# Narrower filler products at the start of a conditioned sequence kernel, and sixty filler products among its last chains

## The chip, the cores and the metric

The kernel runs on one core of a Trainium2 chip. The core has five engines, each with its own in-order queue: TensorE (PE, with weight loads shown apart as PEld), VectorE (DVE), ScalarE (ACT), GpSimd (POOL) and SyncE (SP, which here issues the DMAs). The metric is the device time of one execution in microseconds (us), lower is better.

## The reference

Four layers follow each other on x of 8 batches by 512 tokens by 256 channels, all in float32:

```python
# layer 0: a conditioned transformer block, 16 heads of 16, feed-forward of 1024
emb = jax.nn.silu(_sin_emb(timestep)) @ W_ada + b_ada
scale, shift = jnp.split(emb[:, None, :], 2, axis=-1)
x = _ln(src) * (1.0 + scale) + shift
q, k, v = (heads(x @ W + b) for W, b in ((Wq, bq), (Wk, bk), (Wv, bv)))
scores = jnp.einsum('bhqd,bhkd->bhqk', q / math.sqrt(HEAD_DIM), k) + attention_bias
scores = jnp.where(src_mask, -jnp.inf, scores)
ctx = jnp.einsum('bhqk,bhkd->bhqd', jax.nn.softmax(scores, axis=-1), v)
x = x + (ctx @ Wo + bo)
h = _ln(x) * g2 + beta2
x = x + _gelu2(h @ W1 + b1) @ W2 + b2
# layer 1 and layer 3: adapters of width 64 with an expert chosen by the batch's domain
hidden = gelu(x @ down_W.T + down_b)
hidden = hidden @ expert_W[idx].T + expert_b[idx] + domain_emb[idx]
x = _ln(hidden @ up_W.T + up_b + x) * ln_gamma + ln_beta
# layer 2, between the adapters: pairs of channels turned by the angles theta and phi
```

(`heads` stands for the split into 16 heads. The attention bias, 8 x 16 x 512 x 512 values, is the largest input, 134 MB.)

## The kernel before

The work of each batch is a preparation (layer norm, q, k and v of 512 tokens), 16 attention units (4 groups of four heads by 4 tiles of 128 queries), and a `finish` for tokens (output product, feed-forward, the two adapters with the rotation between them). `finish` takes two tiles of 128 tokens at a time; the last two tiles of the last batch go one by one.

The kernel does not emit instructions as it goes. Each step is given to a `Plan` as a task: an engine (or several to choose from), an estimated cost in us, a function that emits it, what it reads and writes, and a rank. At the end `plan.run` plays the tasks through a model of the engines: whenever an engine is free it takes the ready task of the lowest rank whose buffers can be had. The order so found is the order of every engine's queue; on the chip the engines then wait for each other by semaphores. A filler task therefore fills what the plan believes to be an idle stretch, and stands in PE's queue ahead of whatever comes next. `Buffer(BG)` takes one of four PSUM banks for background work (it may borrow one of the four banks of the scores) and holds it from its first task to its last.

Two places matter here.

At the start, `embedding` (L411) gives PE 42 filler products of the identity with itself at rank -2.45, behind the real work of the first microseconds in rank: L421. Each loads a 128 x 128 weight tile and streams the 128 columns of the same tile. The real work among them is, in PE's order: the tokens spread over the partitions (L429, ready after a small input has landed), a shift of the bias columns (L515), the product of the embedding with w_ada (L484, `product`, four records of 512 columns), the transposes of the first batch (L807), four small transposes of the modulation (L498), then q and k (L827) and the first scores (L936). Five fillers stand before L429, 14 between L515 and L484, 3 before L807, 7 before L827, 6 before the first scores and 7 behind them.

At the end, three `finish` chains overlap: the last batch's tiles 0 and 1 together (A), tile 2 (B) and tile 3 (C). An adapter is a chain of short steps that go from engine to engine: transposes (PE, L751), a copy (L709, ACT or DVE), the down product (PE, L1122), the gelu (ACT, L1130), the up product (PE, L775), the addition (DVE, L1139), statistics (DVE L717 and L719, ACT L731, POOL L724 to L726), the normalized rows (ACT, L739), and either the rotation (DVE L1162, L1158, L1173) or the last scale and shift (DVE, L1149) and the store (L1202). A float32 product leaves two records on PE, each with its own weight load; a transpose leaves one.

Of the kernel before, what the change touches and what calls it, by code (L numbers as in the profile page):

```python
# [20 lines left out]
P = 128  # L21
# [4 lines left out]
NF = FF // P  # L26
# [19 lines left out]
PE, DVE, ACT, POOL, DMA = "PE", "DVE", "ACT", "POOL", "DMA"  # L46
# [202 lines left out]
def conditioned_sequence_kernel(  # L249
# [22 lines left out]
    nc = tc.nc  # L272
# [14 lines left out]
    BG = Slots(banks[4:], SC)  # L287
# [69 lines left out]
    ident = shifted[:, HD:]  # L357
# [28 lines left out]
    plan = Plan()  # L386
# [24 lines left out]
    def embedding():  # L411

        tiny = Buffer(GT)
        tokf = lambda: tiny.t[:1, 0, : 2 * B]
        scr = Buffer(BG, lambda t: t[:, :128].rearrange("p (r n) -> p r n", r=4))

        plan.rank = -2.45
        warm = Buffer(BG, lambda t: t[:, :P])

        def rows_of_identity():  # L420
            nc.tensor.matmul(warm.t, ident, ident, start=True, stop=True)  # L421

        for i in range(42):
            plan(PE, 0.22 if i > 6 else 0.48, rows_of_identity, [], [warm], mode="full")
        plan.rank = -12.0

        plan.rank = -21.0
        plan(DVE, 0.2, lambda: nc.vector.tensor_copy(tokf(), tok_i), [], [(tiny, 0)], at=3.2)
        plan(PE, 0.3, lambda: nc.tensor.matmul(  # L429
            scr.t[:, 0, : 2 * B], ones, tokf(), start=True, stop=True), [(tiny, 0)], [scr],  # L430
            mode="full")

        def reduced():
            turns, last = scr.t[:, 2, : B + 2], scr.t[:, 3, : B + 2]
            red = tiny.t[:, 1, : B + 2]
            nc.vector.tensor_scalar(
                ang[:, :B], scr.t[:, 0, :B], 40.0, cols[:, C_FREQ : C_FREQ + 1], ALU.mult,
                ALU.mult,
            )
            nc.vector.tensor_scalar(turns, ang, float(1.0 / (2.0 * np.pi)), None, ALU.mult)  # L440
            nc.vector.tensor_scalar(turns, turns, ROUND, ROUND, ALU.add, ALU.subtract)
            nc.vector.scalar_tensor_tensor(red, turns, -TWO_PI_HI, ang, ALU.mult, ALU.add)
            nc.vector.scalar_tensor_tensor(red, turns, -TWO_PI_LO, red, ALU.mult, ALU.add)
            nc.vector.tensor_scalar(last, red, PI_IN, -PI_IN, ALU.min, ALU.max)

        plan(DVE, 1.2, reduced, [], [scr, (tiny, 1)], at=4.0)

        def sines():
            red = scr.t[:, 3, : B + 2]
            nc.scalar.activation(sc[:, 0], red, AF.Sin)  # L450
            nc.scalar.activation(sc[:, 1], red, AF.Sin, scale=0.5)
            nc.scalar.activation(sc[:, 1], sc[:, 1], AF.Square)
            nc.scalar.activation(sc[:, 1], sc[:, 1], AF.Identity, bias=1.0, scale=-2.0)

        plan(ACT, 0.9, sines, [scr], ["sc"])

        th = Buffer(BG, lambda t: t[:, : NC * B].rearrange("p (c b) -> p c b", c=NC))
        plan(ACT, 0.25, lambda: nc.scalar.activation(
            th.t, sc[:, :, :B], AF.Tanh, scale=0.5), ["sc"], [th])
        plan(DVE, 0.2, lambda: nc.vector.scalar_tensor_tensor(  # L460
            emb, th.t, 1.0, sc[:, :, :B], ALU.add, ALU.mult), [th, "sc"], ["emb"])
        plan.rank = -11.5

        def chosen():
            domf, clip = scr.t[:A, 0, B : 2 * B], tiny.t[:A, 2, :B]
            nc.vector.tensor_scalar(clip, domf, 0.0, float(E - 1), ALU.max, ALU.min)
            nc.vector.tensor_tensor(valid, domf, clip, ALU.is_equal)
            nc.vector.tensor_tensor(invalid, domf, clip, ALU.not_equal)
            nc.vector.tensor_copy(expert_i, clip[:1])

        plan(DVE, 0.6, chosen, [], [scr, (tiny, 2), "valid", "expert"])
# [264 lines left out]
    def normed(dst, dst_keys, src, src_keys, ts, rstd):  # L736

        for t, key, dkey in zip(ts, src_keys, dst_keys):
            plan(ACT, 0.5, lambda t=t: nc.scalar.activation(  # L739
                dst(t), src.t[:, t, :], AF.Identity, bias=rstd.t[:, 1, t : t + 1],  # L740
                scale=rstd.t[:, 0, t : t + 1]), [rstd, key], [dkey])
# [305 lines left out]
    def feed_forward(res, rk, ts, store=None):  # L1047
        hat = Buffer(TMP)
        at = {t: i for i, t in enumerate(ts)}
        n, w = len(ts), len(ts) * P  # L1050
        here = slice(ts[0], ts[0] + n)

        hk = [(hat, i) for i in range(n)]
        normed(lambda t: hat.t[:, at[t], :], hk, res, rk, ts, statistics(res, rk, ts))
        hT, hk = half_transposed(
            lambda t: hat.t[:, at[t], :], hk, ts, C_G2, C_BETA2
        )
        gT = Buffer(GT) if store is None else store
        for f2 in range(NF // 2):
            ps = Buffer(BG, lambda t: t.rearrange("p (i q) -> p i q", i=2))  # L1060
            sg = Buffer(SIG)
            for i in range(2):
                f = 2 * f2 + i

                def hidden(i=i, f=f, ps=ps):
                    for c in range(NC):
                        nc.tensor.matmul(  # L1067
                            ps.t[:, i, :w], w1[:, c, f * P : (f + 1) * P], hT.t[:, c, :w],
                            start=(c == 0), stop=(c == NC - 1),
                        )  # L1070

                plan(PE, 0.432 * n, hidden, [*hk, "w1"], [(ps, i)], mode="full")

            for i in range(2):
                f = 2 * f2 + i
                plan(ACT, 0.155 + 0.1 * n, lambda i=i, f=f, ps=ps, sg=sg: nc.scalar.activation(  # L1076
                    sg.t[:, i, :w], ps.t[:, i, :w], AF.Tanh, bias=b1s[:, f : f + 1],
                    scale=0.851), [(ps, 0), (ps, 1), "b1s"], [(sg, i)])
            plan(POOL, 0.05 + 0.27 * n, lambda sg=sg: nc.gpsimd.tensor_scalar(  # L1079
                sg.t[:, :, :w], sg.t[:, :, :w], 0.5, 0.5, ALU.mult, ALU.add), [], [(sg, 0), (sg, 1)])  # L1080
            for i in range(2):
                f = 2 * f2 + i
                plan(DVE, 0.14 + 0.13 * n, lambda i=i, f=f, ps=ps, sg=sg: nc.vector.scalar_tensor_tensor(  # L1083
                    gT.t[:, f, :w], ps.t[:, i, :w], cols[:, C_B1 + f : C_B1 + f + 1],
                    sg.t[:, i, :w], ALU.add, ALU.mult), [(ps, i), (sg, i)], [(gT, f)])
        ps = Buffer(BG, lambda t: t.rearrange("p (i d) -> p i d", i=2))
        for i in range(n):
            for f0 in range(0, NF, 2):

                def out_sums(i=i, f0=f0):  # L1090
                    for f in (f0, f0 + 1):
                        nc.tensor.matmul(  # L1092
                            ps.t[:, i, :], gT.t[:, f, i * P : (i + 1) * P], w2[:, f, :],
                            start=(f == 0), stop=(f == NF - 1),
                        )

                plan(PE, 0.86, out_sums, [(gT, f0), (gT, f0 + 1), "w2"], [ps], mode="full")
        plan(DVE, 0.3 * n, lambda: nc.vector.tensor_tensor(
            res.t[:, here], ps.t[:, :n], res.t[:, here], ALU.add), [ps], rk)

    eus, rots = {}, {}

    def adapter(b, l, res, rk, ts):
        n, w = len(ts), len(ts) * P
# [104 lines left out]
    def experts_matrices():  # L1209
# [70 lines left out]
        for b in range(B) for half in range(2) for g in range(NG) for i in range(2)  # L1280
    ]
    embedding()
    modulation()
    constants()
# [5 lines left out]
    for n, u in enumerate(units):  # L1290
        if n % 16 == 0 and u[0] + 1 < B:
            plan.begin()
            prepare(u[0] + 1)
            plan.end(n + 0.5, n + 13.0)
        attention(u, n)
        if n % 8 == 7:
            half = n // 8 % 2
            if n + 1 < len(units):
                plan.begin()
                finish(u[0], [2 * half, 2 * half + 1])  # L1300
                plan.end(n + 2.0, n + (11.0 if n < 100 else 19.0))
                continue

            for t in range(2):
                plan.begin()
                finish(u[0], [2 + t], Buffer(PT, lambda p: p.rearrange(
                    "p (c q) -> p c q", q=2 * P)[:, :NF]) if t else None)
                plan.end(n + 2.0 + 4 * t, n + 11.0 + 4 * t)
    plan.stir([
        (691236, 48.0, 53.0, 0.3),  # L1310
        (61640, 125.7, 135.7, 0.15),
# [135 lines left out]
```

## Time and profile before

| what | us |
|---|---|
| median of 3 runs (lowest to highest) | 879.17 (878.11 to 880.26) |
| the profiled execution's own time | 876.14 |
| its span, first to last instruction | 874.3 |
| mean granted TensorE clock over the span | 0.991 |
| start of L484's first record, end of its chain piece | 10.35, 12.23 |
| start of the first scores (L936) | 19.51 |
| start of the last transposes (L751), down product (L1122), up product (L775) | 863.71, 864.86, 866.42 |
| end of the last DVE operation (L1149) | 871.49 |

The granted clock is the share of TensorE's clock pulses that are let through; it is recorded when it changes, and 1.00 stands where nothing was recorded. In this execution it is recorded as full from 9.52, half from 132.40 to 135.81, full again, and half from 862.85 on. PE matmul records overlap: a record of 128 columns lasts 0.27 us at full clock while the next starts 0.11 behind it, so spacings and not durations tell the pace. A row of the timeline merges equal instructions that follow each other without a gap, with their number as "xN" and, in brackets, the idle time before the first and what ended it.

### The profile page before, as it was taken

Reading aid. Unit: us, or ns where it says so; the run is one execution under the profiler, and the core shown is the slowest. Engines: PE = TensorE matmul, PEld = TensorE weight load, DVE = VectorE, ACT = ScalarE, POOL = GpSimd, SP = SyncE. Lnnn points to the kernel's source line nnn. Section 1 sums busy time; section 2 is a strip of 40 time slices with the busy share of each in tenths; the row PEclk is TensorE's granted clock in tenths of the full one; section 3 lists DMA queues with packets and bytes.
Section 4 is the critical chain, followed back from the end, with each engine's and each line's share of the span. In section 5 each row is a group of like instructions: output and inputs, shape, how many; then the busy total and the mean of one; then the engine's idle time right before and its main releaser. Section 6 shows DMA issues by size and latency. Waiting matters only on the chain.

```text
span 874.3 us, 20269 instructions
## 1 busy us (share of the span) xinstructions
PE 852.1 (97%) x6430; PEld 564.5 (65%) x6430; DVE 784.2 (90%) x2147; ACT 737.1 (84%) x1343; POOL 775.3 (89%) x907
## 2 busy tenths in 40 slices
PE   9999999999999999999999999999999999999994
PEld 7656665667666665667656666666756576666783
DVE  3778998989999989999999989999989899999766
ACT  5997869989898889979899898989989898799653
POOL 8699999989899989999999998998979998999432
PEclk9999999999999999999999999999999999999997
DMA  9689796698888889798897979979887988998300
GB/s 304 208 297 306 262 283 200 200 298 258 281 279 271 263 253 314 217 285 277 286 295 226 301 225 275 314 228 294 269 284 232 279 259 281 299 322 264 98 25 24
DMA packets 163936, 221.56 MB, mean 253 GB/s; under 512 B 18819, under 2 KB 93613, under 8 KB 163782
## 3 DMA queue, kind: packets, MB, share of 16 engines
q1 hardware_dynamic: 163786, 220.25, 79.9%
q8 instruction: 51, 0.84, 0.4%
q14 instruction: 55, 0.45, 0.2%
q10 hardware_dynamic: 44, 0.02, 0.0%
HBM read 152.92 MB, written 7.27 MB: 183 GB/s over the span
## 4 chain that ended last, share of the span: by engine, by line
PE 66%; ACT 13%; POOL 10%; DVE 4%; DMA 3%; issue 3%; SPq 0%; POOLq 0%; DVEq 0%; ACTq 0%
PE bank L936 11%; PE bank L987 10%; PE bank L1092 10%; PE bank L1013 9%; PE bank L1067 8%; POOL bias L928 8%; PE bank L775 5%; PE bank L827 4%; ACT bias L952 4%; DMA bias<-in_bias 3%; PE bank L865 3%; PE bank L751 2%; PE bank L421 2%; PE bank L1122 1%; DVE bias L948 1%
## 5 line engine op out<-in xcount | busy, mean ns | idle before, releaser
L928 POOL TENSOR_TENSOR bias<-bias,neg 128x512 f32<-128x512 f32 x512 | 580.2, 1163 | 10.6 <-DMA bias<-in_bias 9.7
L952 ACT ACTIVATE bias<-bias,low 128x512 f32<-128x512 f32 x512 | 344.9, 719 | 43.7 <-DVE low L948 42.9
L948 DVE CUSTOM_DVE_ANT_0 bias<-bank,bias 128x512 f32<-128x512 f32 x512 | 329.0, 679 | 28.6 <-PE bank L936 21.6
L987 PEld LDWEIGHTS bank<-shifted,bias 128*128 128x128 f32 x1120 | 126.0, 141 | 70.6 <-ACT bias L952 26.0
L963 DVE STREAM_TRANSPOSE tb<-bias 128x512 f32<-128x512 f32 x232 | 156.8, 695 | 7.5 <-ACT bias L952 7.3
L987 PE MATMUL bank<-shifted,bias 128*128 128x128 f32 x1120 | 158.7, 277 | 1.9 <-ACT pT L709 0.7
L936 PE MATMUL bank<-kT,qz 32*128 32x512 f32 x1024 | 146.3, 641 | 3.9 <-DVE low L948 3.8
L709 ACT COPY pT<-bank 128x512 f32<-128x512 f32 x215 | 120.5, 582 | 30.3 <-PE bank L987 29.5
L1067 PE MATMUL bank<-hT,w 128*128 128x256 f32 (+1 forms) x544 | 127.0, 374 | 1.7 <-ACT hT L761 1.2
L1013 PE MATMUL bank<-pT,v_pad 128*32 128x256 f32 x1120 | 123.4, 382 | 0.0
L1092 PE MATMUL bank<-w,gT 128*128 128x256 f32 x496 | 119.9, 383 | 0.0
L1067 PEld LDWEIGHTS bank<-hT,w 128*128 128x128 f32 x544 | 94.1, 190 | 29.5 <-issue 9.0
L1013 PE MATMUL bank<-pT,v_turn 128*32 128x256 f32 x928 | 111.4, 382 | 0.0
L1092 PEld LDWEIGHTS bank<-w,gT 128*128 128x128 f32 x496 | 89.5, 190 | 21.4 <-issue 9.9
L1013 PEld LDWEIGHTS bank<-pT,v_turn 128*32 128x32 f32 x928 | 48.9, 109 | 51.6 <-issue 8.0
L936 PEld LDWEIGHTS bank<-kT,qz 32*128 32x128 f32 x1024 | 40.0, 182 | 43.6 <-DVE low L948 15.0
L1076 ACT ACTIVATE sig<-bank,b1s 128x256 f32<-128x256 f32 (+1 forms) x136 | 55.5, 455 | 8.7 <-PE bank L1067 7.4
L1083 DVE SCALAR_TENSOR_TENSOR gT<-bank,cols,sig 128x256 f32<-128x256 f32 (+1 forms) x128 | 54.2, 464 | 6.5 <-POOL sig L1079 5.9
L1079 POOL TENSOR_SCALAR sig<-sig 128x512 f32<-128x512 f32 (+1 forms) x68 | 40.4, 595 | 20.1 <-ACT sig L1076 17.7
L1013 PEld LDWEIGHTS bank<-pT,v_pad 128*32 128x32 f32 x1120 | 54.8, 109 | 4.4 <-issue 0.8
L717 DVE BATCH_NORM_STATS2 st<-res 128x6 f32<-128x256 f32 x128 | 51.4, 411 | 1.6
L709 DVE COPY pT<-bank 128x512 f32<-128x512 f32 x65 | 43.3, 674 | 5.4 <-ACT bias L952 3.0
(138 smaller groups left out, 1112.5 us busy)
## 6 DMA issues: line engine op xcount, KB each, us to landing
bias<-in_bias SPq DMA_DIRECT2D x512, 256.0 KB
pT<-tb SPq DMA_DIRECT2D x464, 128.0 KB
out<-res SPq DMA_DIRECT2D x15, 256.0 KB
res<-in_x SPq DMA_DIRECT2D x7, 512.0 KB
value_rows<-v_pad SPq DMA_DIRECT2D x8, 272.0 KB
v_turn<-value_rows SPq DMA_DIRECT2D x8, 272.0 KB
m<-in_mask SPq DMA_DIRECT2D x8, 256.0 KB
mod<-ada_rows SPq DMA_DIRECT2D x8, 256.0 KB
```

The source lines that it names most:

```text
L709: nc.scalar.copy(*pair()) if e == ACT else nc.vector.tensor_copy(*pair())), r, w)
L928: plan(POOL, 1.12, lambda j=j: nc.gpsimd.tensor_tensor(dif[j].t, dif[j].t, negs[qt].t, ALU.add), [negs[qt]], [dif[j]])
L936: nc.tensor.matmul(sc[j].t, qz.t[strip, par, c, qs], kT.t[strip, c, :], start=True, stop=True,)
L948: plan(DVE, 0.61, lambda j=j: nc.vector.tensor_tensor_reduce(dif[j].t, sc[j].t, dif[j].t, -1.0, 3.0e38, ALU.add, ALU.min, low.t[:, j : j + ...
L952: plan(ACT, 0.62, lambda j=j: nc.scalar.activation(dif[j].t, dif[j].t, AF.Exp, bias=low.t[:, j : j + 1], scale=-1.0), [(low, j)], [dif[j]] ...
L963: plan(DVE, 0.62, lambda j=j: nc.vector.transpose(tb.t.rearrange("p (m h k c) -> h p k m c", m=4, h=TURNED, k=NT)[j], dif[j].t.rearrange(" ...
L987: nc.tensor.transpose(ps.t[:, kc, :], dif[j].t[:, kc * P : (kc + 1) * P], ident)
L1013: nc.tensor.matmul(pv.t[32 * j : 32 * j + 32, :], (v_turn if j < turned else v_pad).t[:, at : at + 32], pj, start=(kc == 0), stop=(kc == N ...
L1067: nc.tensor.matmul(ps.t[:, i, :w], w1[:, c, f * P : (f + 1) * P], hT.t[:, c, :w], start=(c == 0), stop=(c == NC - 1),)
L1076: plan(ACT, 0.155 + 0.1 * n, lambda i=i, f=f, ps=ps, sg=sg: nc.scalar.activation(sg.t[:, i, :w], ps.t[:, i, :w], AF.Tanh, bias=b1s[:, f : ...
L1083: plan(DVE, 0.14 + 0.13 * n, lambda i=i, f=f, ps=ps, sg=sg: nc.vector.scalar_tensor_tensor(gT.t[:, f, :w], ps.t[:, i, :w], cols[:, C_B1 + ...
L1092: nc.tensor.matmul(ps.t[:, i, :], gT.t[:, f, i * P : (i + 1) * P], w2[:, f, :], start=(f == 0), stop=(f == NF - 1),)
```

## The change

The fillers 7 to 19 of the 42 at the start stream 64 columns of the identity instead of 128, with the same weights and the same planned cost. At the end of the plan, 60 products of the identity with 64 of its columns are added, with the highest rank of all (200.0) and a planned cost of 0.11, ready once the last feed-forward (chain C) has written the last of its activations. They share one bank.

```diff
-        def rows_of_identity():
-            nc.tensor.matmul(warm.t, ident, ident, start=True, stop=True)
+        def rows_of_identity(w):
+            nc.tensor.matmul(warm.t[:, :w], ident, ident[:, :w], start=True, stop=True)
 
         for i in range(42):
-            plan(PE, 0.22 if i > 6 else 0.48, rows_of_identity, [], [warm], mode="full")
+            w = P // 2 if 6 < i < 20 else P
+            plan(PE, 0.22 if i > 6 else 0.48, lambda w=w: rows_of_identity(w), [], [warm],
+                 mode="full")
...
         gT = Buffer(GT) if store is None else store
+        inner.append(gT)
...
-    eus, rots = {}, {}
+    eus, rots, inner = {}, {}, []
...
+    still = Buffer(BG, lambda t: t[:, : P // 2])
+
+    def half_of_identity():
+        nc.tensor.matmul(still.t, ident, ident[:, : P // 2], start=True, stop=True)
+
+    plan.rank = 200.0
+    for _ in range(60):
+        plan(PE, 0.11, half_of_identity, [(inner[-1], NF - 1)], [still], mode="full")
```

In the changed program's queues, PE's real instructions stand in the same order as before, and so do those of DVE, ACT, POOL and SP; only the banks of the last chains differ. Between L515 and the w_ada product stand two full and twelve narrow fillers, behind it one narrow and two full. The sixty stand as follows among the last products (line numbers of the kernel before):

```
L751  transposes of A (adapter 1), then of C (adapter 0)
   7 fillers
L1122 down product of C, then of A
   1
L775  up product of C;  L751 transposes of B (adapter 1)
   2
L775  up product of A;  L1122 down product of B
   6
L775  up product of B
  25
L751  transposes of C (adapter 1)
   7
L1122 down product of C
   6
L775  up product of C
   6
```

## The prediction

> **What bounds the kernel now.** First view: the page's engine totals and slices. TensorE (PE) is busy 97% of a span of 874.3 us and nines in 39 of 40 slices; what delays PE's first real work or its last chain shows in the end time, and little else does.
>
> ```profile
> PE 852.1 (97%) x6430; PEld 564.5 (65%) x6430; DVE 784.2 (90%) x2147; ACT 737.1 (84%) x1343; POOL 775.3 (89%) x907
> PEclk9999999999999999999999999999999999999997
> ```
>
> Second view: the chain of waits in the first 24 us (start, length, what; "xN" counts PE records, and a float32 product leaves two, each with its own weight load).
>
> ```profile
> 1.40 2.50 PE bank L421 x10
> 3.90 0.53 PE bank L429 x2
> 4.44 0.53 PE bank L515 x2
> 4.96 5.46 PE bank L421 x28
> 10.42 1.81 PE bank L484 x4
> ...
> 18.24 1.34 PE bank L421 x12
> ```
>
> The fillers (L421) themselves are the chain: the last input of the product at L484, `emb`, is written by DVE at 7.26 to 7.41, yet L484 follows the 14 fillers at 10.42. They are slow there: a window of 1 us holds 6 filler records at 5.2 and at 8.2 but 11 at 14.5, so a record takes 0.2133 us on the half clock and 0.1117 (18.24: 1.34/12) on the full one. The clock column reads 1.00 before its first change, so durations must tell: the records' starts close up at 9.52. From there it holds until 132.40, falls to half for exactly 3.41 us, and falls again at 862.85. Those times lie a whole number of steps of 3.413 us apart, so I read the clock as decided once per such window, with edges at 2.69, 6.11, 9.52, 12.93. Third view, busy time by window (columns: PE, PEld, DVE, ACT, POOL, clock, DMA):
>
> ```profile
> 2.69:6.11 3.42, 3.42 (x16) 3.16 (x16) 2.40 (x12) 1.79 (x6) 3.09 (x12) 1.00 0.87 231
> 6.11:9.52 3.41, 3.41 (x18) 3.41 (x18) 1.54 (x12) 1.78 (x9) 2.22 (x7) 1.00 1.09 375
> 128.99:132.40 3.41, 1.55 (x12) 0.71 (x11) 2.87 (x8) 2.60 (x6) 3.33 (x6) 1.00 0.90 285
> 753.63:757.04 3.41, 2.26 (x20) 1.29 (x17) 3.38 (x9) 3.41 (x7) 3.17 (x4) 1.00 0.98 310
> ```
>
> The first kept PE "busy" throughout and its weight loads 92%, and did not raise the clock; 1.06 us of it (3.90 to 4.96) were the narrow products L429 and L515. The second, full of wide fillers, did. The third lost the clock, the fourth kept it. Counting a record's moving columns at 0.83 ns each (128 take the 0.1067 that L807's spacing of 0.109 contains), doubled while cold, the moving side streams 65%, 100%, 36% and 56% of these four windows.
>
> Fourth view, the last chain in the timeline (start, length):
>
> ```profile
> 857.53 0.30 PEld L775 LDWEIGHTS bank<-eu,hid 65*128 65x128 f32 x2 [0.26 <-ACT hid L1130]
> 858.22 0.20 PEld L751 LDWEIGHTS bank<-shifted,res 128*128 128x128 f32 x2 [0.39 <-DVE res L1173]
> 863.71 0.69 PE L751 MATMUL bank<-shifted,res 128*128 128x128 f32 x2 [2.36 <-DVE res L1173]
> 864.86 1.11 PE L1122 MATMUL bank<-hT,wd 128*64 128x128 f32 x4 [0.46 <-ACT hT L709]
> 866.42 1.22 PE L775 MATMUL bank<-eu,hid 65*128 65x256 f32 x2 [0.45 <-ACT hid L1130]
> ```
>
> PE waits 2.36, 0.46 and 0.45 us for DVE and ACT, and at half clock its last product takes 1.22 where the same one took 0.70 at 860.65.
>
> **The price of a narrow filler.** A filler loads 128 weight columns and streams 128 (before) or 64. Which side sets the pace? Weight loads of this plain kind take 190 ns (L1067, 128 columns), 137 (L686, 64), 109 (L1013, 32), 88 (L484, 8): 83 ns plus 0.83 per column, so a load occupies its path 107 ns for 128 columns. In the tail, two L775 loads of 0.19 fit in 0.30 (the second 0.11 behind); two transposes' loads (L751, 142 ns) in 0.20, 0.06 behind. Through the whole trace no plain full-height load of 128 columns is followed sooner than 0.108. So the filler's weights already set its 0.1117 (the transposes L807, whose loads are quicker, reach 0.109). Halving the moving side should leave 0.1117 warm (0.223 an instruction) and 0.2133 cold. The cold rows agree: L429 and L515 stream 16 and 8 columns behind 128 weight columns, and their loads last 308 and 310 ns. The other bound is half, 0.112 an instruction (L1267: 64 by 64, eight records in 0.63). I take the first: the filler's weight load is L1067's, not L1267's.
> The Trainium skill (TensorE: Matmul & The Clock Gate, Back-to-back issue gap) gives an isolated product with 1 to 64 moving columns about 60 cycles, half its figure for 128; by it the narrow filler halves. The same passage adds that in a stream of load and product pairs both sides set the spacing.
>
> **The change, part by part.**
> *Order.* All engines keep the order of their real instructions to the end; PE alone gets new instructions, no DMA moves or is added. Two full and twelve narrow fillers stand before the w_ada product, one narrow and two full behind it. The bank that the 60 hold shifts the tail's other banks. The waits that this brings end before they are met (on PE: DVE's reads of a shared bank, done at 857.70 and, in the sum below, 859.7, with PE there at 858.6 and 860.5; on ACT: copies that end by 856.5): nothing.
> *Start, issue time.* 28 records stay 28 cold records: 4.96 + 28 x 0.2133 = 10.93.
> *Start, clock.* The narrow ones stream 64 columns of each 0.1117 (0.2133 cold): 48 to 50%. 65% was not enough, so I expect no rise at 9.52, where the last wide records gained the 0.5 between 10.42 and 10.93. The next edge is 12.93. If it rises there, the product runs 2.0 us cold (2.34 of 4 records at 0.853) and 1.66 x 0.43 warm, ending at 13.65 against 12.23: +1.4. If only at 16.35, product 3.41, three fillers 1.3 and most of eight transposes run cold: the transposes end at about 17.0 against 13.97: +3.1. Everything up to the first scores hangs on this: the transposes L498 need its sum, modc, xT, q, k follow. I take +2.5; bounds 0 (the clock rises as before) and +3.4 (other positions of the edges). At half price the fillers end at about 8.5 (4.96 + 4 x 0.2133 + 24 x 0.1117), `emb` being there; the product then runs half of itself cold, ends near 10.9 and leaves -1.3. Nothing absorbs either: POOL's only early pause, 6.6 us before 35.77, waits for DVE statistics queued behind these scores.
> The Trainium skill (the same page, What's actually happening) has the clock follow some 3.4 us of sustained activity; gapless narrow fillers would satisfy that, and the start would cost 0. The row 2.69:6.11 speaks against reading it so.
> *Tail.* In PE's queue stand 7 narrow fillers ahead of L1122's pair, then 1, 2, 6, 25 before the last transposes, 7 before the last down product, 6 before the last up product, 6 after. The planner counts 0.11 each; at 0.223 the 54 ahead of the last product take 12.06. The real products among them take 0.82 + 0.43 + 0.22 + 0.85 + 0.43 + 0.43 + 0.22 + 0.43 = 3.83. From 855.81 that makes 871.7, 871.9 with exposed loads. Inputs arrive sooner: the last transposes' input, DVE's addition, moves from 863.65 to about 865.5 (the product before it is late by 1.75), while the 25 fillers end at 868.45. The last product then takes 0.70 for 1.22: done at 872.6 against 867.66, **+5.0**. Behind it DVE, POOL, ACT and the output go as before. At half price the fillers fit the waits, except some 0.6 late before the transposes, and the warm clock returns 0.9: -0.3.
> Does the clock hold there? 48% lies between 56% (held) and 36% (lost); it is nearer the first, so I take held. If lost at an edge near 866.3, 5.7 us more of work doubles: tail +11.
>
> *Sum.* +2.5 + 5.0 = +7.5: the profiled execution would go from 876.14 (span 874.3 and 1.84 around it) to 883.6. The runs' median lies 3.03 above the profiled one, so 879.17 + 7.5 = **886.7**.
>
> **Rivals.**
> 1. Clock at the start indifferent to narrow fillers, tail as above: +5.0, 884.2. For: PE has no gap; against: the 65% window.
> 2. The clock is also lost in the tail: +2.5 + 11, about 892.7. Decided by whether 48% holds it.
> 3. The other side: a narrow filler costs half. Start -1.3, tail -0.3: 877.6, down to 877. It decides at about 0.13 us an instruction, where the tail's fillers just fill the waits. For: L1267's 0.056 a record; against: the 0.108 floor of the loads.
> 4. The change does nothing (a rise at the next edge and shorter overlaps cancel): 879.2.
>
> **How the numbers follow.** Forecast 0.48 (own range 885 to 888.5: tail 5.0, start 1.4 to 3.4, run spread 1); rival 1: 0.17; rival 2: 0.20; rival 3: 0.09; rival 4: 0.06. A measurement here tells some 0.2%, 1.8 us, from no change. Rival 3 is split at 877.4, so faster 0.07; the same 0.08; slower 0.85. Leaving out rivals 3 and 4 and the top of 2: 883 to 893.
>
> **What would show it.** L421's narrow records 0.2133 apart until past 10.4 and the first clock record later than 9.6; L1315's records 0.11 apart, PE without a wait from 856, the last product starting near 872 instead of 866.4 relative to an unshifted tail, and clock full until then. Wrong if narrow records stand 0.056 (warm) or 0.107 (cold) apart: then the time falls.

## The result, and the profile after

| | before | after |
|---|---|---|
| median of the runs compared (lowest to highest), us | 877.09 (875.37 to 880.26), 7 runs | 883.76 (881.98 to 886.55), 7 runs |
| ratio after to before, 95% interval | | 1.0081 [1.0066, 1.0096] |
| span of the profiled execution, us | 874.3 | 881.9 |
| its own time, us | 876.14 | 883.76 |

The change costs 0.0081 x 877.09 = 7.1 us (5.8 to 8.4). The two profiled executions differ by 7.6. In the changed kernel the line numbers are some two or three higher: L421 stays, the narrow product L515 is L517, w_ada L484 is L486, the first transposes L807 are L809, the first scores L936 are L938, and in the tail L751, L1122, L775 are L753, L1125, L777; the sixty new fillers are L1315.

The page's engine totals and clock slices of the changed kernel:

```profile
PE 865.6 (98%) x6550; PEld 578.7 (66%) x6550; DVE 784.2 (89%) x2147; ACT 736.7 (84%) x1343; POOL 774.9 (88%) x907
PEclk9999999999999999999999999999999999999999
```

PE has 120 records more, two for each of the sixty, and the last slice no longer shows the half clock that the kernel before had there. The clock was bought, and the time rose all the same.

The chain of waits at the start of the changed kernel (start, length, what):

```profile
5.24 6.07 PE bank L421 x28
11.30 3.51 PE bank L486 x4
14.81 1.27 PE bank L421 x6
16.09 0.87 PE bank L809 x8
16.96 0.34 PE bank L500 x4
...
22.57 1.07 PE bank L938 x8
```

and two rows of the same chain before:

```profile
13.10 0.87 PE bank L807 x8
...
19.58 1.07 PE bank L936 x8
```

The 28 filler records take as long as 28 wide ones would on the half clock (0.2133 apart), and the product L486 behind them takes 3.51 us where it took 1.81. The transposes end at 16.96 instead of 13.97, the first scores start at 22.57 instead of 19.58 on the same chain: 2.99 us later both, 0.28 of it because the row of fillers began that much later in this execution (5.24 for 4.96). Most of the delay lasts: PE's next two longer pauses end at 51.79 and 134.60, against 48.80 and 131.74 before, and one at 758.70 against 756.00. By the next, which ends at 807.25 against 805.23, it is down to 2.02; what took the last 0.7 off in this execution the runs do not show.

Busy time by window of the changed kernel (columns: window, its length, PE, PEld, DVE, ACT, POOL, clock, DMA share, GB/s; the clock column shows 1.00 where nothing was recorded yet, the first record is at 15.64):

```profile
5.40:8.81 3.41, 3.41 (x18) 3.41 (x17) 2.34 (x16) 1.16 (x7) 1.93 (x7) 1.00 1.03 344
8.81:12.22 3.41, 3.41 (x14) 2.54 (x14) 0.00 (x0) 3.26 (x7) 2.69 (x10) 1.00 1.04 378
12.22:15.64 3.42, 3.42 (x8) 1.03 (x6) 0.68 (x1) 0.90 (x2) 2.81 (x3) 1.00 0.91 341
865.56:868.97 3.41, 3.41 (x33) 3.41 (x32) 3.10 (x9) 1.23 (x3) 1.39 (x5) 1.00 0.00 0
868.97:872.38 3.41, 3.41 (x34) 3.41 (x32) 0.64 (x2) 0.84 (x2) 0.00 (x0) 1.00 0.23 77
```

PE is busy without a break in all five. The first two, in which moving columns stream 61% and 62% of the time, do not raise the clock; the third, with the wide product and 85%, does, at its end. The last two, at 48% and 51%, keep a clock that is already full.

The tail of the changed kernel in the timeline, PE alone (start, length, line, tile, shape, records):

```profile
857.17 0.82 PE L753 MATMUL bank<-shifted,res 128*128 128x128 f32 x6
...
863.41 1.55 PE L1315 MATMUL bank<-shifted 128*128 128x64 f32 x12
864.80 0.65 PE L777 MATMUL bank<-eu,hid 65*128 65x256 f32 x2
865.29 5.69 PE L1315 MATMUL bank<-shifted 128*128 128x64 f32 x50
870.82 0.39 PE L753 MATMUL bank<-shifted,res 128*128 128x128 f32 x2
871.04 1.67 PE L1315 MATMUL bank<-shifted 128*128 128x64 f32 x14
872.64 0.65 PE L1125 MATMUL bank<-hT,wd 128*64 128x128 f32 x4
873.23 1.55 PE L1315 MATMUL bank<-shifted 128*128 128x64 f32 x12
874.62 0.65 PE L777 MATMUL bank<-eu,hid 65*128 65x256 f32 x2
```

The first row holds the transposes of A and C; before it was

```profile
855.15 0.82 PE L751 MATMUL bank<-shifted,res 128*128 128x128 f32 x6
```

No row of the changed kernel has a bracket: PE waits for nothing. From these transposes to the last product's start it takes 17.45 us, against 11.27 before (855.15 to 866.42). The 50 records start 0.1106 apart (870.82 less 865.29, over 50), the pace of a wide record. The input of the transposes L753 was written by DVE from 867.33 to 867.75, so this real work stood 3.1 us behind fillers. The last product takes 0.65 instead of 1.22; from its end (875.27) to the end of the span there are 6.6 us, as before (867.64 to 874.3). The gain of the full clock is 0.57 us; the price of keeping it, 6.18 us in this pair of executions, is ten times that. 6.18 less 0.57, and the 2.02 us left of the start, make the 7.6 between the two.

### The profile page after: what moved, and what is told of

Same layout as the page of the kernel before. It is cut to its first block, busy times and chain, and to the rows that moved or that the text cites. A ratio compares the mean times of both kernels' runs of the same rounds, so it can differ in the third digit from the quotient of the medians.

```text
span 881.9 us, 20511 instructions
## 1 busy us (share of the span) xinstructions
PE 865.6 (98%) x6550; PEld 578.7 (66%) x6550; DVE 784.2 (89%) x2147; ACT 736.7 (84%) x1343; POOL 774.9 (88%) x907
## 4 chain that ended last, share of the span: by engine, by line
PE 60%; ACT 14%; POOL 11%; DVE 7%; DMA 4%; issue 3%; SPq 0%; ACTq 0%; POOLq 0%; DVEq 0%
PE bank L938 10%; PE bank L989 9%; PE bank L1095 9%; POOL bias L930 8%; PE bank L1070 8%; PE bank L1015 7%; ACT bias L954 5%; PE bank L777 4%; PE bank L829 4%; PE bank L867 2%; DVE bias L950 2%; DMA bias<-in_bias 2%; PE bank L753 2%; PE bank L1125 1%; PE bank L1315 1%
## 5 line engine op out<-in xcount | busy, mean ns | idle before, releaser
L938 PE MATMUL bank<-kT,qz 32*128 32x512 f32 x1024 | 146.5, 642 | 3.8 <-DVE low L950 3.8
L938 PEld LDWEIGHTS bank<-kT,qz 32*128 32x128 f32 x1024 | 40.0, 183 | 43.5 <-DVE low L950 14.9
```

The costliest lines, as they stand in the source:

```text
L938: nc.tensor.matmul(sc[j].t, qz.t[strip, par, c, qs], kT.t[strip, c, :], start=True, stop=True,)
```

## The experiments

Three questions stood open: whether the weight load or the moving side sets a filler's pace, what raises and what keeps the clock, and whether the two halves of the change are worth what the sum gave them. The kernels ran in four groups, each with its own runs of the kernel before on the same chip: medians 876.33 (25 runs), 876.75 (35), 876.51 (17) and 876.36 (13).

| run | median, us (runs) | ratio to before | 95% interval |
|---|---|---|---|
| start_only | 878.31 (11) | 1.0023 | [1.0014, 1.0032] |
| tail_only | 882.64 (5) | 1.0068 | [1.0054, 1.0082] |
| start_w64_n64 | 873.72 (9) | 0.9975 | [0.9962, 0.9988] |
| start_w64_n128 | 876.70 (11) | 1.0001 | [0.9988, 1.0014] |
| tail_w64 | 877.05 (12) | 0.9998 | [0.9987, 1.0010] |
| tail_cost22 | 876.79 (12) | 0.9991 | [0.9977, 1.0005] |
| start_none | 874.73 (12) | 0.9978 | [0.9966, 0.9990] |
| all_w64_tail_w64 | 874.15 (12) | 0.9974 | [0.9961, 0.9987] |
| tail_k32 | 894.00 (4) | 1.0188 | [1.0157, 1.0219] |
| none_cost22 | 875.61 (12) | 0.9976 | [0.9964, 0.9988] |
| tail_w16 | 877.88 (10) | 1.0021 | [1.0009, 1.0032] |

### The halves alone

**start_only**: the change without its last part (the edit against the changed kernel).

```diff
-    plan.rank = 200.0
-    for _ in range(60):
-        plan(PE, 0.11, half_of_identity, [(inner[-1], NF - 1)], [still], mode="full")
```

> The narrow fillers of the start alone, without the sixty at the end. Theory (128 weight columns set the pace, and streaming 64 of 128 columns is too little for the clock to rise): narrow records 0.2133 us apart, first rise of the clock after 12 us, w_ada product over at 13.7 to 14.8 instead of 12.2; time +2.2 to +3.2 us against before (ratio 1.0025 to 1.0037). Rival A (the start costs nothing, all of the loss is in the tail): 0. Rival B (a narrow filler costs half): -1.3 us.

Measured +2.0 us (0.0023 x 876.33; 1.2 to 2.8), a little under the range expected. The chain of waits of start_only:

```profile
4.98 6.07 PE bank L421 x28
11.04 3.51 PE bank L486 x4
14.56 1.41 PE bank L421 x6
15.96 0.87 PE bank L809 x8
```

It is the start of the full change, 0.26 earlier: transposes done at 16.84, 2.87 later than before, the clock full at 15.66. The narrow fillers alone keep it down.

**tail_only**: the sixty at the end, the start as before (against the changed kernel).

```diff
-        def rows_of_identity(w):
-            nc.tensor.matmul(warm.t[:, :w], ident, ident[:, :w], start=True, stop=True)
+        def rows_of_identity():
+            nc.tensor.matmul(warm.t, ident, ident, start=True, stop=True)
...
-            w = P // 2 if 6 < i < 20 else P
-            plan(PE, 0.22 if i > 6 else 0.48, lambda w=w: rows_of_identity(w), [], [warm],
-                 mode="full")
+            plan(PE, 0.22 if i > 6 else 0.48, rows_of_identity, [], [warm], mode="full")
```

> The sixty products at the end alone, the start as before. Theory (a product costs 0.223 where the plan has 0.11, and the clock holds): PE without a wait from 856 on, last up product starts about 5.5 us later than before, time +4.5 to +5.2 us (ratio 1.0051 to 1.0059). Rival A (they hide in the waits as planned; the loss came from the start): 0 to -0.5. Rival C (start and tail do not add, the tail alone also shows the start's loss): +7.

Measured +6.0 us (4.7 to 7.2), above the 4.5 to 5.2 expected. The timeline of tail_only, PE:

```profile
857.71 0.82 PE L751 MATMUL bank<-shifted,res 128*128 128x128 f32 x6
...
865.83 5.69 PE L1313 MATMUL bank<-shifted 128*128 128x64 f32 x50
871.36 0.39 PE L751 MATMUL bank<-shifted,res 128*128 128x128 f32 x2
...
875.15 0.65 PE L775 MATMUL bank<-eu,hid 65*128 65x256 f32 x2
```

From the transposes of A and C (855.15 before, 857.71 here) to the last product's start it takes 17.44 us here and 11.27 before: +6.17, less 0.57 for the shorter last product, +5.6. The two halves sum to 8.0, inside the change's own 5.8 to 8.4.

### What sets a filler's pace

**start_w64_n64** and **start_w64_n128**: the fillers 7 to 19 load 64 weight columns and stream 64 (the diff), or load 64 and stream 128 (with (64, 128) in its place); the sixty are left out. This edit and the following ones stand against the kernel before, or against tail_only where the sixty are in them.

```diff
+        def rows_of_identity(m, n):
+            nc.tensor.matmul(warm.t[:m, :n], ident[:, :m], ident[:, :n], start=True, stop=True)
...
+            m, n = (64, 64) if 6 < i < 20 else (P, P)
+            plan(PE, 0.22 if i > 6 else 0.48, lambda m=m, n=n: rows_of_identity(m, n), [], [warm],
+                 mode="full")
```

> Start alone with fillers 7 to 19 narrow on both sides: 64 weight columns and 64 moving columns, in the same places. Theory (the weight load sets the pace of a narrow filler): records 0.107 apart on the half clock, w_ada product starts near 8.5 and ends near 11; if the clock goes by streamed columns it rises as before, time -0.8 to -1.5 us. Rival D (the clock counts active cells of the array): pace 0.107 too, but the rise comes a window or more later; time -0.5 to +1.5. Rival E (the pace of a filler is not the weight load's): 0.2133 apart as in the change.

> Start alone with fillers 7 to 19 of 64 weight columns and 128 moving columns, in the same places. Pace 0.2133 on the half clock for every theory (128 moving columns). Theory (the clock goes by the share of time in which columns stream): rises as before, between 8 and 12 us; time 0, within 0.8 us. Rival D (it goes by active cells: half of them): rises after 12 us as in the change; time +2 to +3.2 us.

The chain of waits of start_w64_n64:

```profile
5.07 3.81 PE bank L421 x28
8.88 2.89 PE bank L486 x4
11.77 0.90 PE bank L421 x6
```

and of start_w64_n128:

```profile
4.97 5.94 PE bank L421 x28
10.91 1.81 PE bank L486 x4
```

With 64 weight columns and 64 moving ones the 28 records take 3.81 us; with 128 on either side they take 6.07 (start_only) or 5.94. So a record costs the longer of its two sides, and the narrow filler of the change had kept the long one. The first ends the product at 11.77, before 12.23, and beats the kernel before by 2.2 us (0.0025 x 876.33; 1.1 to 3.3), more than the 0.8 to 1.5 expected. Its profile does not show where the rest comes from: it is that of the slowest of its nine runs (876.77), and its first scores start only 0.44 us earlier than before (19.14). In both runs the clock rose in the window that streamed 96% or 100%. In the second, fillers with half of the weight columns filled that window; in the first the product, with 8 weight columns, filled most of it: the rise does not ask for all columns.

**tail_w64**: the sixty with 64 weight columns.

```diff
-        nc.tensor.matmul(still.t, ident, ident[:, : P // 2], start=True, stop=True)
+        nc.tensor.matmul(still.t[: P // 2], ident[:, : P // 2], ident[:, : P // 2], start=True, stop=True)
```

> The sixty products at the end alone, in the same places, with 64 weight columns and 64 moving columns each; the start as before. Theory (the plan's 0.11 is what a product with 64 weight columns costs; the tail's loss is the other half): records 0.056 apart, the 25 before the last transposes end before or within 0.7 us of their input, clock full to the end of the last product; time -0.8 to +0.4 us against before. Rival F (any filler in the queue ahead of the last chains delays them, whatever its pace): +2.5 to +5.

The timeline of tail_w64, PE:

```profile
855.87 0.82 PE L751 MATMUL bank<-shifted,res 128*128 128x128 f32 x6
...
862.76 3.13 PE L1313 MATMUL bank<-shifted 128*64 128x64 f32 x50
865.82 0.44 PE L751 MATMUL bank<-shifted,res 128*128 128x128 f32 x2
...
868.28 0.70 PE L775 MATMUL bank<-eu,hid 65*128 65x256 f32 x2
```

0.061 a record, the clock full to 873.43, and the loss is gone (0.9998). It is also no gain: from the transposes of A and C (855.87) to the last product's start it takes 12.41 us against 11.27 before, and the last product at full clock gives back 0.52 of these 1.1.

**tail_cost22**: thirty of the sixty, planned at what they cost.

```diff
-    for _ in range(60):
-        plan(PE, 0.11, half_of_identity, [(inner[-1], NF - 1)], [still], mode="full")
+    for _ in range(30):
+        plan(PE, 0.224, half_of_identity, [(inner[-1], NF - 1)], [still], mode="full")
```

> Products with 128 weight columns and 64 moving columns at the end alone, 30 of them, planned at 0.224 instead of 0.11; the plan puts 3, 1, 1, 3, 12, 3, 3 and 4 where it had 7, 1, 2, 6, 25, 7, 6 and 6. Theory (the loss comes from the planned price being half of the real one): time -0.6 to +0.8 us against before, with the clock full to the end of the last product if 48% streamed holds it. Rival F (fillers ahead of the chains cost time whatever is planned): +2 to +3.

The timeline of tail_cost22, PE:

```profile
857.48 0.82 PE L751 MATMUL bank<-shifted,res 128*128 128x128 f32 x6
...
863.87 2.79 PE L1313 MATMUL bank<-shifted 128*128 128x64 f32 x24
866.50 0.39 PE L751 MATMUL bank<-shifted,res 128*128 128x128 f32 x2
...
868.73 0.65 PE L775 MATMUL bank<-eu,hid 65*128 65x256 f32 x2
```

Narrow products as such do no harm: with the right planned cost 24 records stand where 50 stood, from the transposes of A and C (857.48) to the last product's start it takes 11.25 us (11.27 before), and the time is that of before within the interval (0.9991). Twice too many of them for the pauses is what made the tail long. The edit changed the planned cost and the number of fillers at once; that the plan put about half as many into each gap points to the cost.

### Are the fillers worth anything

**start_none**: the fillers 7 to 19 issue nothing.

```diff
-            plan(PE, 0.22 if i > 6 else 0.48, rows_of_identity, [], [warm], mode="full")
+            plan(PE, 0.22 if i > 6 else 0.48,
+                 (lambda: None) if 6 < i < 20 else rows_of_identity, [], [warm], mode="full")
```

> Start alone with fillers 7 to 19 emitting nothing, the rest in the same places: what the thirteen are worth. Theory: the w_ada product starts near 7.6 on the half clock and ends near 11; no window before it is streamed enough, so the rise comes near or after 12 us in spite of the early product; time -1.0 to +1.0 us against before, and so 1 to 3 us faster than the narrow ones. Rival (the thirteen fillers are needed to raise the clock in time, wide or narrow): +2 us or more.

The chain of waits of start_none:

```profile
7.46 0.08 DVE emb L461
7.54 0.04 issue
7.58 3.34 PE bank L485 x4
10.92 0.64 PE bank L421 x4
```

The product now follows its own input, `emb`, and not the fillers, and the kernel is 1.9 us faster than before (0.0022 x 876.75). The expected cost of a late rise did not come: the clock rose at 10.54, since the cold product alone streams 87% of the window 7.13 to 10.54. The product raises the clock as well as a filler does, and it is work.

**all_w64_tail_w64**: all fillers of the start from the sixth on, and the sixty, with 64 weight and 64 moving columns.

```diff
+            nc.tensor.matmul(warm.t[:m, :m], ident[:, :m], ident[:, :m], start=True, stop=True)
...
+            m = P if i < 5 else P // 2
...
+        nc.tensor.matmul(still.t[: P // 2], ident[:, : P // 2], ident[:, : P // 2], start=True, stop=True)
```

> Every filler of the start from the sixth on with 64 weight columns and 64 moving columns, in the same places, and the sixty of the tail likewise. Theory: the fillers behind the product, which outlast the inputs they wait for by 0.4 to 0.8 us in the profile before, end in time as well; together with the start's -2.2 measured with thirteen of them and about 0 in the tail: -3 to -5 us against before. Rival G (the later fillers hide, or the clock falls back with half of the array used): -1 to -2.5.

The chain of waits of all_w64_tail_w64 has the first scores 2.5 us earlier than before:

```profile
17.05 1.08 PE bank L938 x8
```

The time fell by 2.3 us (0.0026 x 876.75; 1.1 to 3.4), short of the 3 to 5 of the theory and within the rival's. In the profile PE's pauses come 3.1 to 3.3 us sooner up to 752.66, and the span is 871.8, 2.5 less. The other 0.6 goes in the tail, as in tail_w64: from the transposes of A and C (852.05) to the last product's start (864.46) it takes 12.41 us against 11.27, and the last product gives back 0.52. The theory had put about 0 there.

**none_cost22**: the start of start_none and the tail of tail_cost22.

```diff
+                 (lambda: None) if 6 < i < 20 else rows_of_identity, [], [warm], mode="full")
...
+    for _ in range(30):
+        plan(PE, 0.224, half_of_identity, [(inner[-1], NF - 1)], [still], mode="full")
```

> The start of start_none and the thirty narrow products of tail_cost22, planned at 0.224 each, in one kernel. Theory: the start gives 2.0 us as it did alone (start_none 0.9978), the tail 0 to 0.8 us as it did alone (tail_cost22 0.9991): 874 to 874.8 us beside a before of 876.75, ratio 0.997 to 0.998. Rival: the filler-free start lets the tail's gain come out in full, as the pauses before it do not hide it: below 873.5, ratio under 0.9963.

Measured 875.61, ratio 0.9976: 2.1 us less, the start's gain again. The tail's 0.57 does not show, but it would be lost in the interval (1.1 to 3.2 us less). Its median lies 0.8 above the range that the theory gave, its ratio in it; the rival (the tail's gain comes out in full) lies just outside the interval. Four versions beat the kernel before by 0.22% to 0.26%, and their intervals overlap so far that the runs rank none of them first.

### What keeps the clock

The prediction had the share of time in which moving columns stream decide, for the rise and for keeping. The rise agreed in every trace. Keeping did not: start_only lost the clock in a window with a share of 0.53 (862.16 to 865.57), while the full change kept it at 0.48. In the first, three quarters of the streaming is that of L777, whose products sum over 65 of 128 rows (six records of 0.21 us, beside four of 0.11). Busy time in that window of start_only:

```profile
862.16:865.57 3.41, 2.44 (x12) 1.40 (x11) 2.99 (x9) 1.71 (x5) 1.21 (x5) 1.00 0.00 0
```

**tail_k32**: tail_only, with 32 rows of the identity in the sum.

```diff
-        nc.tensor.matmul(still.t, ident, ident[:, : P // 2], start=True, stop=True)
+        nc.tensor.matmul(still.t, ident[:32], ident[:32, : P // 2], start=True, stop=True)
```

> Sixty narrow products as in tail_only, but with 32 rows of the identity in the sum instead of 128 (32 x 128 weights, 64 moving columns), so the share of the window in which columns stream stays 0.48 and the share of the array's cells that they use falls to a quarter. Theory H (what keeps the full clock is the share of streamed columns): the clock holds to the last product, 50 records of the longest stretch in 5.4 to 5.7 us, time as tail_only, 881 to 884 us. Rival I (what keeps it is the share of streamed columns weighted by the cells in use; the windows that lost the clock had at most 0.35 by this count and these would have 0.12 to 0.2): the clock falls one window into the long stretch, between 868 and 872, the records after it stand 0.21 apart, and the time rises to 885 to 890 us.

The timeline of tail_k32, PE:

```profile
865.35 1.64 PE L1313 MATMUL bank<-shifted 32*128 32x64 f32 x12
866.92 1.22 PE L775 MATMUL bank<-eu,hid 65*128 65x256 f32 x2
868.07 10.93 PE L1313 MATMUL bank<-shifted 32*128 32x64 f32 x50
...
886.51 1.22 PE L775 MATMUL bank<-eu,hid 65*128 65x256 f32 x2
```

The clock fell at 866.66, and the 50 records take 10.93 us. The window before that, in the same view of busy time by window:

```profile
863.25:866.66 3.41, 3.41 (x24) 2.79 (x24) 2.45 (x8) 1.39 (x4) 0.95 (x3) 1.00 0.00 0
```

PE was busy in all of it. A clock lost with no pause at all, at a streamed share of 0.61: theory H falls. The rival's mechanism stands, its price was too small: +16.5 us, since the clock fell earlier than it had supposed and none of the later windows (0.49 to 0.57 streamed) could raise it again. But rows were changed here, and not columns, so the count could go by cells (rows times weight columns) or by rows alone.

**tail_w16**: 16 weight columns on all 128 rows.

```diff
-        nc.tensor.matmul(still.t, ident, ident[:, : P // 2], start=True, stop=True)
+        nc.tensor.matmul(still.t[:16], ident[:, :16], ident[:, : P // 2], start=True, stop=True)
```

> Sixty narrow products that load 16 weight columns of all 128 rows and stream 64 (tail_w64 with a quarter of its weight columns). Tells apart two readings of why tail_k32 lost the clock. Theory J (the streamed share counts by the rows of the array that it feeds: in the traces so far every full-clock window above 0.37 by this count kept the clock and every one below 0.35 lost it, and cold windows rose above 0.77 and not below 0.74): the fillers stream some 0.8 to 0.9 of a window on all rows, the clock holds to the last product, records 0.055 to 0.06 apart, time as tail_w64, 876 to 878 us. Rival I (it counts by cells, rows times weight columns: 0.1 to 0.2 here): the clock falls between 863 and 869, the last product takes 1.2 instead of 0.7, time 879 to 883 us.

The timeline of tail_w16, PE:

```profile
861.45 2.97 PE L1313 MATMUL bank<-shifted 128*16 128x64 f32 x50
...
866.96 0.70 PE L775 MATMUL bank<-eu,hid 65*128 65x256 f32 x2
```

The clock stayed full to 872.57 on a quarter of the cells of tail_w64: theory J. The median, 877.88, is in the range given, though over the kernel before (by the ratio 1.8 us, 0.8 to 2.8). The profiled execution has 0.8 of it in the tail: from the transposes of A and C (854.36) to the last product's start it takes 12.60 us against 11.27, and the last product gives back 0.52.

Worked out from the traces, for a window of 3.413 us (moving columns x 0.83 ns, doubled at half clock, over the window; "by rows" weighs each product with the share of the 128 rows that it feeds, "by cells" with rows and weight columns; products that overlap count once in "streamed" and each in the other two):

```
run              window           streamed  by rows  by cells  clock
tail_only          4.06 to   7.47   0.75     0.74     0.74     stays half
after              8.81 to  12.22   0.62     0.63     0.34     stays half
start_w64_n128   133.21 to 136.63   0.90     0.89     0.89     rises
after             12.22 to  15.64   0.85     0.85     0.20     rises
start_none         7.13 to  10.54   0.87     0.88     0.05     rises
tail_k32         863.25 to 866.66   0.61     0.31     0.25     lost
start_only       862.16 to 865.57   0.53     0.34     0.28     lost
start_w64_n64    127.06 to 130.47   0.47     0.35     0.35     lost
tail_cost22      867.61 to 871.02   0.43     0.37     0.33     kept
after            865.56 to 868.97   0.48     0.48     0.48     kept
tail_w16         865.74 to 869.15   0.59     0.53     0.16     kept
```

Of some 3,300 windows in the 13 traces, counted by rows, every one at full clock that lost it has 0.35 or less and every one that kept it 0.37 or more; at half clock none rose at 0.74 or less, and all rose at 0.85 or more. (The 0.77 in what was expected of tail_w16 comes from the window of start_w64_n128 in this table, with four products that began 0.05 us before its edge counted at full clock; nearly all of their streaming was at half clock.) The count by rows was found in the traces and then tried on one new run, tail_w16; the bounds are no finer than the count itself, which takes each product's streaming from its columns.

## Why the prediction was right

**What bounds.** Right in the main: the 2.99 us of the start were still 2.70 at 758.70 and 2.02 at 807.25, against a prediction that nothing absorbs them, and the fillers, with real work ready behind them at both ends, were the chain.

**The price of a narrow filler.** Right, and the base of all the rest: 0.2133 us a record cold (at half clock) and 0.1106 warm (at full clock). The proof is start_w64_n64: halving the weights too brings 3.81 us for 6.07. The bound of half, and with it rival 3, falls.

**Start, issue time.** 10.93 was given, 11.04 and 11.30 came; the second is the later begin.

**Start, clock.** The term was +2.5 within 0 to 3.4; alone it measured +2.0 (1.2 to 2.8), in the chain +2.99. Neither of the two edges named (12.93 and 16.35) came, since they continue the steps of the execution before: in this one the edges fall at 8.81, 12.22 and 15.64, and the rise came at 15.64. In the kernels that kept the wide fillers it came anywhere from 8.99 (tail_w16) to 10.89 (tail_only); such a shift from one execution to the next may be why runs of one kernel spread over 4 us; that was not tried by itself. The trace's 2.99 and the runs' 2.0 need not agree, since a delay still changes behind the start: at the transposes of A and C it was 2.02 in the changed kernel (857.17 for 855.15), while in start_only 2.87 had become 3.76 (858.91). That narrow fillers do not raise the clock was right; rival 1 (+5.0) lies below the measured 5.8 to 8.4, and start_only's interval leaves out zero.

The Trainium skill (TensorE: Matmul & The Clock Gate, What's actually happening) has the full clock come after about 3.4 us of sustained activity. By it the fillers of 5.24 to 11.30 would have raised the clock by 12.22. Here the measurement decides: PE busy in the whole of two windows, and no rise.

**Tail.** +5.0 was given, +6.0 (4.7 to 7.2) came, and 5.6 in the profile of tail_only. From first filler to the last product's start it took 16.79 us, where the sum had 16.1 (855.81 to 871.9). The missing 0.7 is hardly in the fillers, whose 50 records take the 5.53 us that 0.1106 makes and whose 108 take 12.17 for 12.06, but in the real products, 4.62 us where the sum had 3.83 and 0.2 of exposed loads: each change from filler to product and back costs some hundredths more than the spacing of like records (12 records of L1125 hold PE from 859.43 to 860.45, 1.02, where the sum had 0.82). The 54 fillers before the last product, the 3.1 us by which ready transposes stood behind them, and the 0.65 for the last product (0.70 in the sum) were close to the prediction.

**The clock in the tail.** Held, as taken; rival 2 falls for this change. The reason was half right: 0.48 is above the bound, but the bound counts rows, and the reading from 36% (lost) and 56% (kept) held here only because the products of the identity feed all 128. tail_k32 is rival 2 come true, at +16.5 instead of +11.

**Sum.** +7.5 was given and +7.1 (5.8 to 8.4) came; the profiled execution was to take 883.6 and took 883.76. That this agrees within 0.2 is luck: in this pair of executions the start left 2.02 for 2.5 and the tail 5.61 for 5.0, and the two misses cancel. The predicted 886.7 is 2.9 above the median, and the median lies below the forecast's own range of 885 to 888.5 and nearer to the 884.2 of rival 1; the difference to the kernel before, the late rise and start_only speak for the forecast. The number is off because of one term: the median of three runs stood 3.03 above the profiled execution, that of all seven only 0.95. Rival 4 falls with the interval.

## What to carry to other kernels

A filler is priced by the longer of its two sides, weight load and moving columns; narrow one alone and it costs the same, while a planner that is told half will put twice as many ahead of real work. To warm or hold the clock count what streams on how many rows, not how busy the engine looks, and first see whether the real work, started sooner, does it by itself: here leaving thirteen fillers out gained as much (0.22%) as halving them on both sides (0.25%). A gain of a last product at full clock (0.57 us) has to be set against what stands before it in the queue.

## What the hardware showed that was not expected

- Full weight loading does not raise the clock: windows with loads in 100% (5.40 to 8.81 of the changed kernel) and 99% (tail_only, 4.06 to 7.47) of the time did not raise the clock at streamed shares of 0.61 and 0.75.
- The clock can be lost without a pause: tail_k32, 863.25 to 866.66, PE busy 3.41 of 3.41 us, by rows 0.31.
- To raise the clock takes about twice what keeps it: between 0.74 and 0.85 by rows against between 0.35 and 0.37. Work between the two stays in the state it finds: the changed kernel's start at 0.61 stayed at half clock, its tail at 0.48 at full clock.
- Weight columns do not count: 16 of them on all rows kept the clock (tail_w16, by cells 0.16), and the product of start_none raised it at 0.05 by cells.

Open stays whether the 0.57 us of a last product at full clock can be had in the timed runs. In tail_cost22, whose profile has the gain at no loss ahead of it, the time changed by -0.8 us with an interval from -2.0 to +0.4, which agrees with the gain and with none; the intervals here are too wide for it. Open is also where the rest of tail_w16's loss lies, some 1 us beside the 0.8 in its tail.
